# Attention block of a transformer layer: query projection as 4x4 by 4x4 blocks in 49 products, computed for all tokens ahead of the attention

## The chip, the cores and the metric

The kernel runs on one core of one Trainium2 chip. A core has a matrix engine (TensorE, PE in the profile), a vector engine (VectorE, DVE), an activation engine (ScalarE, ACT), a general engine (GpSimd, POOL) and a sync engine (SyncE, SP) that here only issues DMA transfers. Each engine works through its own instructions in order; semaphores tie them together. The metric is device time in microseconds (us), lower is better. The kernel before takes 1169.54 us, the median of three runs (1169.38 to 1170.08).

## The reference, cut to what matters

All arithmetic is fp32. There are 16 sequences of 128 tokens and a model width of 1024. Attention has 32 query heads of 32 columns in 8 key/value groups, so keys and values are 256 columns wide each.

```python
# _layernorm(x) = (x - mean) / sqrt(var + 1e-5)
h = _layernorm(x)                      # (16, 128, 1024)
query = h @ w_q.T                      # 1024 columns
key   = ctx @ w_k.T                    # 256 columns
value = ctx @ w_v.T                    # 256 columns
scores = einsum('bghnd,bgsd->bghns', query, key) / 32 ** 0.5
attention = softmax(where(mask, scores, finfo.min))
out = einsum('bghns,bgsd->bghnd', attention, value)
x = x + out @ w_out.T
h2 = _layernorm(x)
x1, x2 = split(h2 @ w12.T + b12)       # 2 x 1024 columns
x = x + (silu(x1) * x2) @ w3.T + b3
```

## The kernel before

**Tokens.** The 2048 tokens are two halves `T` = 0 and 1 of 1024 tokens (8 sequences `t` each). One half is two column blocks of 512 tokens, the widest matmul the kernel uses.

**Products in seven.** Every projection is a product of a 2x2-block left operand (weights) with a 2x2-block right operand (tokens), done by Winograd's scheme with 7 block products instead of 8. `seven_right` (L217) makes the differences of the right operand: four of shape 128x1024 in two pieces each, some on VectorE, the late ones on VectorE or GpSimd. `left_sums` (L245) makes the four sums of the left operand on GpSimd. `seven` (L263) runs the products in a given order: for each product a chain of matmuls into one PSUM bank (`chain`, L186), then the eviction. It uses four banks. Product 1 is copied by ScalarE (`p1`, L275), products 6 and 5 become `u1` and `u3` by two VectorE additions (L278, L280), and the result blocks come out by `done`. After each product `hook(j)` starts whatever is planned there: loads, sums, differences, statistics.

**Rounds.** `seven_round(T, k, R)` (L481) is one round: 7 products of 4 matmuls, 28 matmuls, each 128x128 weights by 128x512 tokens. Round `k` = 0 makes the keys of half `T`, `k` = 1 its values, `k` = 2 to 5 its queries, a quarter of the query columns each. The query weights are centred and scaled first (`centre`, L438), so that only 1/std of the layer norm is left for the scores. The centred weights are stored to DRAM and read again for half 1. `O_round(r)` (L605) is the output projection of two sequences, also 28 matmuls, with the residual added by `into` (L596).

**Order.** First the keys and values of half 0, interleaved; then its four query rounds, alone on the matrix engine; then the attention of half 0, and beside it the six rounds of half 1 (keys, values, four of queries); then the attention of half 1, and beside it output rounds 0 to 5. Output rounds 6 and 7, the second layer norm and the feed-forward part follow. `x_work` (L714) feeds the differences of the query rounds, `wo_work` those of the output rounds.

**Attention.** A unit is one sequence `t` and one half of the heads `gh`; a half `T` has 16 units. `scores` (L518) issues 16 small matmuls into four PSUM banks `s`. VectorE scales and masks each bank in place (L535) and takes the row maximum (L538), two banks at a time. ScalarE does 16 exponentials with row sums (L544). VectorE inverts the sums (L550) and GpSimd scales the probabilities `p` (L553). One unit later `flip` (L556) transposes `p` in four groups on the matrix engine, and VectorE copies each group to SBUF (`pT`, L561). Another unit later `values` (L564) multiplies with the values, and ScalarE copies the result (L575).

**How the two are interleaved.** The loop at L778 takes `share` us of round work per unit out of a `Stream` (L75): a quarter after the scores, 0.15 after `values`, 0.15 after each of the four flips. `share` is 147.0/16 in half 0 and (24.1*6 - 18)/16 in half 1. The matrix engine's order is fixed by the program in all parts (`manual_schedule`, L154); in the attention the order on VectorE, ScalarE, GpSimd and SP is chosen by a scheduler when the program is built.

**Buffers.** `psum` (L160) has 8 banks for everything: scores, flips, values and rounds. `units` (L157) has 44 buffers of 128x1024 fp32, `temps` 14 of 128x512. A new tile waits until the last user of its buffer is done.

**Feed-forward.** The product with w12 already uses the seven-product scheme twice: 4x4 by 4x4 blocks in 49 small products. A `step` (L937) is one inner set of 7 products of 2 matmuls. 28 steps go over 7 outer products times 4 groups of output rows. Partial results live in SBUF or in DRAM (`hold`, `store`, `fetch`, L907 to L916), and `gather` (L918) adds one to another with an accumulating DMA issued by GpSimd.

## Time and profile before

The profiled execution took 1167.91 us; its span from the first to the last instruction is 1166.1 us. That is 1.63 us below the median of the runs shown.

| what | where in the span, us |
|---|---|
| keys, values of half 0 | 8.6 to about 58 |
| queries of half 0 | about 58 to 153.0 |
| first scores of half 0 / of half 1 | 153.0 / 366.2 |
| last scores of half 1 | 548.5 |
| first matmul of the w12 steps | 639.3 |
| first matmul with w3 | 983.7 |

Engine totals over the span: PE 1156.3 us (99%), DVE 823.2 (71%), POOL 584.5 (50%), ACT 342.2 (29%). A fp32 matmul of these shapes is two PE instructions in the profile. Busy times of the matrix engine come from modelled ends, so its share says that it had work queued, and the chain of waits says better what it waited for. The granted clock of the matrix engine is 1.000 over the whole span.

### The profile page before, as it was taken

To read this page: it belongs to the slowest core of one execution; us is meant where nothing else is said; L and a number is where in the kernel's file an instruction comes from. 1 tells how busy PE (TensorE), PEld (TensorE's weight loads), DVE (VectorE), ACT (ScalarE), POOL (GpSimd) and SP (SyncE) were. 2 spreads that over 40 slices of the span, in tenths; PEclk is the share of its full clock that TensorE was granted. 3 is DMA by queue.
4 is the path that set the end of the run, shared out by engine and by line. 5 is a ranking of instruction groups with operands and counts; after the bars stand their busy time and mean duration, and the time that the engine had idled before them with its cause. 6 is when DMAs were issued, how large, how long until landed. Compare 5 with 4: busy or idle time off the path is not lost.

```text
span 1166.1 us, 13425 instructions
## 1 busy us (share of the span) xinstructions
PE 1156.3 (99%) x4288; PEld 541.0 (46%) x4288; DVE 823.2 (71%) x1194; ACT 342.2 (29%) x1325; POOL 584.5 (50%) x543
## 2 busy tenths in 40 slices
PE   9999999999999999999999999999999999999998
PEld 4444444444544455454454554444444444444443
DVE  4572368878678888888646446766777787978772
ACT  1120044555544464644261321110011022111111
POOL 5532255745356665556443358562523442548555
PEclk9999999999999999999999999999999999999999
DMA  9674342221215333133475789878834879272411
GB/s 366 249 281 169 125 146 91 91 91 55 91 55 199 127 109 128 55 128 109 162 278 209 277 333 318 231 246 252 173 106 157 221 203 277 91 270 91 162 73 72
DMA packets 65653, 200.13 MB, mean 172 GB/s; under 512 B 7088, under 2 KB 11184, under 8 KB 65584
## 3 DMA queue, kind: packets, MB, share of 16 engines
q1 hardware_dynamic: 60400, 180.93, 42.6%
q0 software_dynamic: 4320, 15.73, 7.2%
q10 hardware_dynamic: 864, 2.62, 0.6%
q8 instruction: 34, 0.56, 0.2%
q14 instruction: 35, 0.29, 0.1%
HBM read 127.95 MB, written 63.96 MB: 165 GB/s over the span
## 4 chain that ended last, share of the span: by engine, by line
PE 92%; DVE 4%; DMA 2%; issue 1%; ACT 0%; POOL 0%; SPq 0%; DVEq 0%; POOLq 0%; ACTq 0%
PE F_b L189 26%; PE Q_b L189 22%; PE O_b L189 17%; PE G_b L189 15%; PE pt L559 4%; PE s L526 3%; PE o L571 2%; PE xt L667 1%; DMA M<-U_dram 1%; DVE wo_T L233 1%; DMA ctx<-in_ctxT_dram 1%; DVE s L535 1%; DVE xT_T L233 1%; DMA OTr<-OT_dram 0%; DVE nmax L538 0%
## 5 line engine op out<-in xcount | busy, mean ns | idle before, releaser
L544 ACT ACTIVATE p<-s,nmax 128x128 f32<-128x128 f32 x512 | 181.4, 407 | 176.2 <-DVE nmax L538 168.7
L553 POOL TENSOR_TENSOR p<-p,inv 128x512 f32<-128x512 f32 x128 | 136.3, 1086 | 168.2 <-DVE inv L550 128.9
L189 PE MATMUL F_b<-X_T,L 128*128 128x512 f32 x304 | 135.7, 592 | 0.0
L544 ACT ACTIVATION_READ_ACCUMULATOR p<-s,nmax 128x1 f32 x512 | 126.3, 247 | 0.0
L189 PE MATMUL G_b<-w_R,A_L 128*128 128x512 f32 x256 | 114.4, 592 | 0.0
L535 DVE SCALAR_TENSOR_TENSOR s<-s,mr,drop 128x512 f32<-128x512 f32 x128 | 90.3, 751 | 24.6 <-PE s L526 24.5
L561 DVE COPY pT<-pt 128x512 f32<-128x512 f32 x128 | 84.4, 676 | 18.1 <-PE pt L559 17.1
L559 PEld LDWEIGHTS pt<-ident,p 128*128 128x128 f32 x512 | 63.6, 141 | 69.8 <-issue 63.5
L189 PEld LDWEIGHTS F_b<-X_T,L 128*128 128x128 f32 x304 | 57.4, 190 | 70.8 <-issue 69.4
L538 DVE TENSOR_REDUCE nmax<-s 128x4 f32<-128x512 f32 x128 | 81.8, 680 | 0.0
L559 PE MATMUL pt<-ident,p 128*128 128x128 f32 x512 | 76.9, 273 | 2.4 <-issue 2.4
L189 PEld LDWEIGHTS G_b<-w_R,A_L 128*128 128x128 f32 x256 | 48.6, 190 | 61.2 <-issue 59.6
L293 POOL TENSOR_TENSOR x<-x,G_n 128x512 f32<-128x512 f32 x36 | 49.9, 1413 | 49.4 <-DVE G_n L356 30.0
L374 ACT COPY G_c<-G_b 128x512 f32<-128x512 f32 x52 | 30.4, 585 | 142.3 <-PE G_b L189 141.1
L275 ACT COPY F_p<-F_b 128x512 f32<-128x512 f32 x28 | 16.4, 585 | 187.5 <-PE F_b L189 187.5
L950 DVE TENSOR_TENSOR M<-F_u,F_b 128x512 f32<-128x512 f32 x57 | 39.0, 685 | 44.8 <-PE F_b L189 43.1
L293 POOL TENSOR_TENSOR x<-x,G_c 128x512 f32<-128x512 f32 x36 | 53.8, 1512 | 32.5 <-ACT G_c L374 16.7
L189 PE MATMUL O_b<-wo_T,O_S 128*128 128x512 f32 x128 | 61.7, 601 | 0.0
L189 PE MATMUL O_b<-wo,O_S 128*128 128x512 f32 x128 | 61.6, 601 | 0.0
L189 PE MATMUL F_b<-xnT,L 128*128 128x512 f32 x128 | 60.8, 592 | 0.0
L189 PE MATMUL Q_b<-xT,wq 128*128 128x512 f32 x128 | 60.1, 597 | 0.0
L189 PE MATMUL Q_b<-xT_T,A_S 128*128 128x512 f32 x128 | 59.9, 598 | 0.0
(209 smaller groups left out, 2055.8 us busy)
## 6 DMA issues: line engine op xcount, KB each, us to landing
w<-in_w_dram SPq DMA_DIRECT2D x36, 512.0 KB, 6.8
xT<-in_xT_dram SPq DMA_DIRECT2D x16, 512.0 KB, 7.9
xs<-in_x_dram SPq DMA_DIRECT2D x16, 512.0 KB, 5.9
xp<-in_x_dram SPq DMA_DIRECT2D x16, 512.0 KB, 6.7
x_dram<-xp SPq DMA_DIRECT2D x16, 512.0 KB, 2.9
xn_dram<-xn SPq DMA_DIRECT2D x16, 512.0 KB, 2.9
xnr<-xn_dram SPq DMA_DIRECT2D x16, 512.0 KB, 5.7
h<-hT_dram SPq DMA_DIRECT2D x16, 512.0 KB, 6.0
```

The costliest lines, as they stand in the source:

```text
L189: nc.tensor.matmul(ps, lhsT, rhs, start=start and i == 0, stop=stop and i == len(pairs) - 1, skip_group_check=True,)
L233: eng.tensor_sub(t[e], a()[e], b()[e])
L293: (eng.tensor_add if op == "+" else eng.tensor_sub)(out, a, b)
L374: nc.scalar.copy(t, ps)
L526: nc.tensor.matmul(ps[gl][:, j, :], QT[T, c, gh * 2 + j // 2][rows, j % 2, toks], KT[T, c][rows, gh, toks], start=True, stop=True,)
L535: nc.vector.scalar_tensor_tensor(s, s, rstd, drop.unsqueeze(1).to_broadcast([P, HPG, S]), ALU.mult, ALU.add,)
L538: nc.vector.tensor_reduce(nmax[:, e], s, AX.X, ALU.max, negate=True)
L544: nc.scalar.activation(p[:, j, :], ps[gl][:, j, :], AF.Exp, bias=nmax[:, e, j : j + 1], accum_out=total[:, e, j : j + 1],)
L553: nc.gpsimd.tensor_mul(p, p, inv[:, e].unsqueeze(2).to_broadcast([P, HPG, S]))
L559: nc.tensor.transpose(pt[:, j, :], p[:, j, :], ident)
L561: nc.vector.tensor_copy(pT, pt)
L950: nc.vector.tensor_add(dst, s, ps)
```

## The change

1. The query rounds go. The queries of all 2048 tokens are made in one piece between the keys and values of half 0 and its attention: weights in 2 groups `g` of 512 query columns, 4x4 blocks of the weights (128 rows each) by 4x4 blocks of the tokens (512 each), 7 outer times 7 inner products. One `q_step` is 7 products of 2 matmuls; there are 14 steps, 196 matmuls.
2. VectorE makes the outer differences of the tokens (`q_outer_right`, 16 of 128x1024) and the inner ones (`q_inner_right`, 28 of 128x1024). All token blocks are loaded once, 16 of 512 KB.
3. GpSimd makes the outer sums of the weights (`q_outer_left`, 8 instructions of 128x512 per group) and the inner ones (`q_inner_left`, 4 of 128x256 per step). Outer sums go through DRAM and come back two steps ahead of their use.
4. Partial results: outer products 1, 2, 3 and 5 have their own tiles; 6, 7 and 4 are added to a tile `u` by two VectorE additions per block. Two sums pass through DRAM (`q_store`, `q_fetch`), and three times per group `q_gather` adds two tiles by an accumulating DMA of GpSimd. Finished queries of half 1 and some of half 0 are stored to DRAM and loaded before their attention (`q_home`).
5. Statistics of half 0 move into the steps, those of half 1 into its key and value rounds and output rounds 0 and 1.
6. Beside the attention of half 0 now run: keys and values of half 1, output rounds 0 and 1. Beside that of half 1: output rounds 2 to 5. `share` becomes 98.0/16 and (24.1*4 - 12)/16.
7. The stage of the steps has its order written out on all five engines; the attention stages keep the scheduler as before.

```diff
+class Pieces:
+    def __init__(self, made):
+        self.made = made
+    def __getitem__(self, k):
+        return [self.made[k]]
...
-    wq_dram = [tc.dram_tile([P, 2, KC, P], F32, name=f"wq_dram_{m}") for m in range(4)]
...
+    OUTER = (1, 2, 3, 6, 5, 7, 4)
+    INNER = (1, 5, 6, 7, 2, 3, 4)
+    Q_STEPS = [(g, i) for i in OUTER for g in range(2)]
+    def load_xq(K, C, h, c):
+        xq[2 * K + h, 2 * C + c] = load(xT[C][2 * K + h, c], [2, 512], f"xq_{2 * K + h}_{2 * C + c}")
+    def q_outer_right(i, h, c):
+        B11, B12, B21, B22 = (xq.get((2 * K + h, 2 * C + c)) for K in range(2) for C in range(2))
+        y = Y.setdefault(i, {})
+        if i in (1, 2, 3):
+            y[h, c] = {1: B11, 2: B21, 3: B22}[i]
+            return
+        out, x, z = {
+            5: (B11, B12, B11), 6: (None, B22, Y.get(5, {}).get((h, c))), 7: (B12, B22, B12),
+            4: (B21, B21, Y.get(6, {}).get((h, c))),
+        }[i]
+        y[h, c] = out if out is not None else unit([2, 512], f"Y6_{h}_{c}")
+        nc.vector.tensor_sub(y[h, c], x, z)
+    def q_inner_right(i, k):
...
+        nc.vector.tensor_sub(r[k], a, b)
+    def q_outer_left(g):
+        A11, A12, A21, A22 = (q_part(g, R, K) for R in range(2) for K in range(2))
+        S = {k: unit([2, 2, 2, P], f"QS{k}_{g}") for k in (5, 6, 7, 3)}
+        for k, a, op, b in (
+            (5, A21, "+", A22), (6, S[5], "-", A11), (3, A12, "-", S[6]), (7, A11, "-", A21),
+        ):
+            for h in range(2):
+                x, z = (t[:, h] if t in (S[5], S[6]) else t[h] for t in (a, b))
+                put(nc.gpsimd, S[k][:, h], x, op, z)
+        for k in (2, 3, 6, 5, 7, 4):
+            t = q_dram[g, k] = tc.dram_tile([P, 2, 2, 2, P], F32, name=f"QS{k}_dram_{g}")
...
+    def q_gather(g, to, frm):
+        for r in range(2):
+            o, x = ((q_sum_dram if k in ("U", "V") else q_sum)[g, k][r] for k in (to, frm))
+            nc.gpsimd.dma_start(o, x, accum_op=ALU.add)
+    def q_step(n):
+        g, i = Q_STEPS[n]
         def done(rc, s, ps):
+            dst, u, v = (q_sum[g, k][rc[0]][:, rc[1]] if (g, k) in q_sum else None for k in (i, "u", "v"))
+            if dst is None:
+                nc.vector.tensor_add(u, u, ps)
+                if s is not None:
+                    nc.vector.tensor_add(u, u, s)
+                return
             if s is None:
                 nc.scalar.copy(dst, ps)
             else:
                 nc.vector.tensor_add(dst, s, ps)
+            if i == 5:
+                nc.vector.tensor_add(v, v, ps if s is None else dst)
...
+    def q_plans():
+        for n, (g, i) in enumerate(Q_STEPS):
+            if i != 1:
+                q_at(n - 2, 3, q_load_left, g, i)
+            for e, k in enumerate((1, 5, 6, 7, 3)):
+                q_at(n - 1, 3 + e if n else min(5 + e // 2, 7), q_inner_left, g, i, k)
...
+            if i == 1:
+                q_at(0 if g else -1, 7, q_outer_left, g)
+                q_at(n + 1, 2, q_store, g, i, "U")
...
+        for i, hcs, ks in (
+            (1, [(-1, 5)] * 4, ((-1, 6), (-1, 6), (-1, 7), (0, 1))),
+            (2, [(0, 6)] * 4, ((0, 7), (1, 1), (1, 2), (1, 7))),
+            (5, [(2, 1), (2, 2), (3, 1), (3, 2)], ((6, 7), (7, 1), (7, 2), (7, 7))),
+            (3, [(2, 6)] * 4, ((2, 7), (3, 4), (3, 7), (4, 4))),
+            (6, [(4, 1), (4, 2), (4, 7), (5, 1)], ((5, 2), (5, 7), (6, 1), (6, 2))),
+            (7, [(8, 1), (8, 2), (8, 7), (9, 1)], ((9, 2), (9, 7), (10, 1), (10, 2))),
+            (4, [(10, 7), (11, 1), (11, 2), (11, 4)], ((11, 7), (12, 1), (12, 2), (12, 4))),
+        ):
...
     def O_round(r):
-        if r + 1 < B // 2:
+        if EARLY <= r < B // 2 - 1:
             load_pair(r + 1)
...
-            if j == 5 and r + 1 < B // 2:
+            tick()
+            if j == 3 and r < EARLY:
+                load_pair(r + 1)
+            if j == (6 if r < EARLY else 5) and r + 1 < B // 2:
                 left_O(r + 1)
+            if r < 2 and j in (1, 3):
+                load_xs(NT + 4 + 2 * r + j // 2)
+            if r < 2 and j in (4, 6):
+                q_stats(NT + 4 + 2 * r + j // 2 - 2)
...
-    stream.add(*(seven_round(0, k, x_R[0]) for k in range(2, 6)))
-    stream.finish()
+    with tc.manual_schedule(engines={ENGINES.PE, ENGINES.DVE, ENGINES.Activation, ENGINES.Pool, ENGINES.SP}):
+        stream.add(*(q_step(n) for n in range(len(Q_STEPS))))
+        stream.finish()
+    feeds["ctx_1"].finish()
...
-            stream.add(*(seven_round(1, k, ctx_R[1] if k < 2 else x_R[1]) for k in range(6)))
-            share = 147.0 / NT / GH
+            stream.add(*(seven_round(1, k, ctx_R[1]) for k in range(2)))
+            stream.add(*(O_round(r) for r in range(2)))
+            share = 98.0 / NT / GH
         else:
-            stream.add(*(O_round(r) for r in range(EARLY)))
-            share = (24.1 * EARLY - 18.0) / NT / GH
+            stream.add(*(O_round(r) for r in range(2, EARLY)))
+            share = (24.1 * (EARLY - 2) - 12.0) / NT / GH
```

A plan entry (n, j) means: in step n, after its product number j; n = -1 is the last of the key and value rounds of half 0.

## The prediction

> **What bounds the kernel now.** I read the chain of waits first, then busy times by stage, then one attention unit in the timeline.

> ```profile
> PE 92%; DVE 4%; DMA 2%; issue 1%; ACT 0%; POOL 0%; SPq 0%; DVEq 0%; POOLq 0%; ACTq 0%
> ...
> 74.96 78.11 PE Q_b L189 x182
> ```
> ```profile
> 58.00:153.00 95.00, 95.00 (x225) 42.00 (x223) 41.87 (x69) 11.46 (x23) 31.87 (x35) 1.00 0.51 184
> 153.00:366.20 213.20, 210.64 (x1221) 104.20 (x1220) 173.43 (x290) 106.66 (x544) 111.45 (x99) 1.00 0.25 88
> 366.20:548.50 182.30, 181.56 (x1117) 89.97 (x1116) 152.01 (x275) 95.86 (x504) 114.35 (x111) 1.00 0.34 126
> ```
> The chain is the matrix engine nearly everywhere. Its second line gives the price of a matmul: 78.11 / 182 = 0.429 us per instruction, two per matmul, 0.858 us. In the stage table the columns are length, then busy PE, weight loads, DVE, ACT, POOL. VectorE is at 44% in the query stage, 81% and 83% in the two attention stages. So the matrix engine leads, with VectorE not far behind beside the attention.

> ```profile
> 451.13 1.17 PE L526 MATMUL s<-K,Q 32*128 32x128 f32 x32
> 452.32 1.42 DVE L535 SCALAR_TENSOR_TENSOR s<-s,mr,drop 128x512 f32<-128x512 f32 x2 [1.25 <-PE s L526]
> ...
> 454.42 0.37 ACT L544 ACTIVATE p<-s,nmax 128x128 f32<-128x128 f32 x1 [2.59 <-DVE nmax L538]
> ...
> 460.30 0.30 ACT L544 ACTIVATION_READ_ACCUMULATOR p<-s,nmax 128x1 f32 x1
> 460.63 0.20 DVE L550 RECIPROCAL inv<-sum 128x8 f32<-128x8 f32 x1 [0.95 <-ACT p L544]
> 460.75 1.24 DVE L561 COPY pT<-pt 128x512 f32<-128x512 f32 x2
> 462.52 0.68 DVE L561 COPY pT<-pt 128x512 f32<-128x512 f32 x1
> 463.11 1.16 PE L526 MATMUL s<-K,Q 32*128 32x128 f32 x30
> ```
> This is one unit of half 1: 463.11 - 451.13 = 11.98 us from scores to scores. From the scores to the end of the last exponential it is 460.60 - 451.13 = 9.47 us, if VectorE is free when the scores come. The slack is 2.5 us. I hold on to it because of the eight banks: in both programs as built, the next unit's scores wait for banks that the last exponentials, or VectorE's copies of the flips, still hold. So 9.47 plus about 0.1 for the semaphore, 9.6 us, is a floor of the unit's period, whatever the matrix engine has to do.

> **The change, part by part.**

> **1. Matmuls: -24.0 us.** Eight query rounds of 28 matmuls go (224), 14 steps of 14 come (196). 28 x 0.858 = 24.0 us. The built programs agree: 2480 matmul instructions before, 2452 after.

> **2. The query stage: +10 us (4 to 25).** It grows from 4 rounds to 14 x 14 x 0.858 = 168.2 us of matmuls. VectorE's work in it: 41 of the 44 differences of 128x1024 (3 come earlier) at 1.65 us, 67.7; `u1` and `u3`, 28 x 0.69 = 19.3; 74 block additions (24 into own tiles, 42 into `u`, 8 into `v`) x 0.69 = 51.1; the eight sequences' statistics (16 x 0.673 + 8 x 0.51) = 14.8; centring of group 1, 8 x 0.61 = 4.9; four differences of the context for the next stage, 6.6. Sum 164.4 us, 98% of the matmuls beside it. It is uneven: steps of outer products 6, 5, 7 and 4 have nine additions (6.2), about three differences (5.0) and, up to step 10, statistics (1.8), 13.0 us against 12.0. The eight steps from number 6 on fall behind by some 7 us. The first six carry 10 us each, but what they save can't be used ahead, since the differences are at fixed places. When outer product 7 begins, its second and third inner difference are made at the end of step 9 and in step 10, directly ahead of the products that use them; a late VectorE is then a waiting matrix engine. The feed-forward steps are the nearest row: 392 x 0.858 = 336.3 in 344.4 us, 8 us lost in 28 steps with VectorE at 68%. Below nothing is excluded: no matmul became shorter. I take 7 for the overload and 3 for the start: SP's stores of the outer sums wait for GpSimd (16 instructions of 1.27 us), and behind them in SP's queue stand the loads of the last token blocks, which VectorE needs in step 2. ScalarE (11%) and the accumulating DMAs (12 of them; 6 to 9 us to landing, with a step or more between) lie under the matmuls; if such a DMA is late by x, VectorE waits x.

> [...]

> ```profile
> L860 DVE TENSOR_TENSOR X_T<-xnT,X_T x12: 1212/1222/3311, 620.6 to 924.9; 128x1024 f32<-128x1024 f32 x12
> L860 DVE TENSOR_TENSOR X_T<-xnT,xnT x10: 1218/1222/3362, 617.1 to 888.9; 128x1024 f32<-128x1024 f32 x10
> ```
> The same difference takes 1.22 us in the middle and up to 3.36 us (min, median, max); the page's means are 1.63 and 1.68. [...] All 44 differences have two SBUF inputs and GpSimd sums weights beside them. Left alone, 44 x 1.22 = 54 us; by the mean row, 73. [...] I take the mean row, since GpSimd is busy about 45% in the feed-forward and about 40% in the new stage.

> **3. Attention of half 0: +21.6 us (5 to 35).** The period was 213.2 / 16 = 13.3 us. 49 us of rounds go: 13.3 - 49/16 = 10.25 us for the matrix engine. VectorE: 173.4, less four token differences (7.8), twelve query blocks (8.0) and two rounds' `u` (2.7), plus eight output blocks (5.4), four more sequences' statistics for the second norm (5.5) and 1 of small ones: 166.8 / 16 = 10.4 us per unit, above the matrix engine's 10.25. Two queues, each full, that wait for each other in order can't both be kept full. What a late VectorE instruction does can be seen:

> ```profile
> 349.96 5.88 DVE L233 TENSOR_TENSOR wo_T<-wo,wo_T 128x1024 f32<-128x1024 f32 x2
> 350.42 1.17 PE L526 MATMUL s<-K,Q 32*128 32x128 f32 x32
> 355.77 0.75 DVE L535 SCALAR_TENSOR_TENSOR s<-s,mr,drop 128x512 f32<-128x512 f32 x1
> ```
> Two differences stand ahead of the masking, which starts 5.35 us after the scores instead of 1.19; that unit took 15.75 us even with today's slack. I take 11.6 us per unit, 1.35 x 16.

> **4. Attention of half 1: +19.5 us (3 to 30).** Period 182.3 / 15 = 12.15. `share` falls from 7.91 to 5.28, so 9.5 us for the matrix engine, already under the floor of 9.6. VectorE: 152.0 less seven output blocks, six statistics and four `u`, 140.5 / 15 = 9.4. I chained four units by hand in the built order of VectorE, with the durations above. Sequence 10, first half: two additions, two statistics and three copies still stand ahead of its masking, which begins 3.3 us after its scores; exponentials end at 11.6; the next scores wait for them: 11.75. Its second half: an inversion that waits for the last exponential (10.45) stands ahead of three copies, to 12.0, and the next scores wait for the third: 12.05. The two units before it come to 9.6 and 9.9. Mean 10.8, 1.3 x 15 = 19.5.

> **5. The rest: 0.** The queries' stores and loads (SP has 435 transfers for 391) land units ahead of use; DMA was at 0.25 and 0.34 beside the attention and 0.51 in the query stage. Should loads wait for one of the 44 buffers, the first output round starts late, 5 us. The tail after the last scores has 12 instead of 18 us of rounds to cover the last flips; these need the last scores' probabilities about 13 us after the scores, and come later than that.

> **Sum.** -24.0 + 10 + 21.6 + 19.5 = +27.1. The profiled execution of 1167.9 becomes 1195.0 (its span 1166.1 becomes 1193.2); with the 1.6 us by which the median lies above it, **1197 us**.

> **Clock.** The granted clock is 1.00 in every row. [...]

> **Rivals.**
> - *The cover holds; faster.* VectorE's queue keeps up, as it did at 83% without visible waits; the mechanism is that banks come free in time because the scheduler puts the masking first. Then half 1 pays only the floor and the flips that wait for exponentials (9.9 - 9.5) x 15 = 6, half 0 only its one unit with differences, 4, the steps 4: -24 + 14 = -10, 1159 us. It wins while the three stages together lose under 24 us. Against it: VectorE's sum per unit already equals the matrix engine's.
> - *The head of the query stage.* SP stands behind GpSimd's outer sums, the token loads land 7 to 8 us late in step 2, VectorE never makes it up: 15 more in that stage, 1212 us. For it: SP's order is written out; against it: the banks of two steps lie between.
> - *The matmuls go but the units overlap badly throughout*: 12.2 us in half 0 and 11.5 in half 1: +31 + 30 + 10 - 24, 1217 us.

> That the change doesn't do what it says is excluded by the count of matmuls.

> **Chances.** The forecast with its bounds (1175 to 1208) 0.53; head of the query stage 0.13; units worse 0.14; faster 0.14; around no change 0.06. Range 1168 to 1224. Within 0.2% (2.3 us) is what a measurement can't tell from no change: 0.04; slower 0.82, faster 0.14.

> **What would show it.** Period between scores: 10.25 or below in half 0 and 9.6 in half 1 says the cover holds; 11 to 12 says I am right. VectorE's share in these stages should be 88 to 95%, and its inversions and masking should end the waits of the matrix engine there. The stage of the steps should last 172 to 193 us, with waits for differences in steps 8 to 13. A granted clock below 0.98 there, or waits for loads, would mean another cause than mine.

## The result, and the profile after

The changed kernel takes **1206.63 us** (median of 4 runs, 1201.86 to 1208.91) against 1169.46 us for the kernel before in the same comparison (4 runs, 1169.17 to 1170.08): 1.031 times the time, 95% interval 1.028 to 1.035. The profiled execution took 1208.91 us, its span is 1207.0 us. The forecast was 1197 us, 1195.0 for the profiled execution, with 1168 to 1224 as the range.

The page of the changed kernel, its busy times and its chain of waits:

```profile
PE 1165.1 (97%) x4232; PEld 540.9 (45%) x4232; DVE 907.4 (75%) x1288; ACT 345.5 (29%) x1331; POOL 623.4 (52%) x575
...
PE 63%; DVE 11%; ACT 7%; DMA 5%; issue 3%; POOL 2%; SPq 0%; ACTq 0%; DVEq 0%; POOLq 0%
```

The matrix engine was 92% of the chain and is now 63%; VectorE and ScalarE, 4% together before, now carry 18%. The matrix engine is busy for 1165.1 us although 28 matmuls are gone: before it was 1156.3. So its instructions have become longer somewhere. The stage table (start:end, length, busy time of PE, weight loads, DVE, ACT and POOL, granted clock, DMA share, GB/s) shows where: query stage, attention of half 0, attention of half 1.

```profile
57.95:247.10 189.15, 175.92 (x401) 75.99 (x399) 155.59 (x188) 17.54 (x34) 96.08 (x89) 0.96 0.83 279
247.10:433.37 186.27, 172.48 (x1106) 87.03 (x1105) 160.76 (x286) 103.16 (x538) 106.68 (x99) 0.96 0.34 125
433.37:594.88 161.51, 154.16 (x1023) 76.30 (x1022) 141.38 (x261) 93.51 (x496) 86.42 (x89) 0.97 0.22 83
```

The third number from the end is the granted clock, as a share of full speed. It was 1.00 in every row before; now it is 0.96 to 0.97 in all three stages that the change touches, and 1.00 in the rest. The mean over the span is 0.984: as the clock in the records is either full or half, 2 x 0.016 x 1207 = 39 us of the span ran at half clock (37.5 us in six stretches, and the very end).

| stage | before | forecast | measured |
|---|---|---|---|
| query stage | 95.0 | 178.2 | 189.15 |
| attention, half 0 (16 periods) | 213.2 | 185.6 | 186.3 |
| attention, half 1 (15 periods) | 182.3 | 162.0 | 161.5 |
| from the last scores to the end | 617.6 | 609.4 | 612.1 |

The forecast of the last row is what is left of the forecast span of 1193.2 us after the others and the first 58 us.

The two stages of attention came out as forecast, to 0.7 us. But they are not made as forecast. The periods from scores to scores, read off the starts of the score matmuls in the timeline, are:

```
half 0:  8.2 11.0 11.2 10.3 10.3 11.3 17.8 10.7 10.2 12.1 10.4 11.5 10.3 10.7 10.4 20.0
half 1: 10.5 10.6 10.0  9.4 11.0 11.1 12.4 10.3  9.6  9.9 16.2  9.6 10.8  9.9 10.2
```

Most units are near the matrix engine's own 10.25 us in half 0 and near the floor of 9.6 us in half 1; three long units of 17.8, 20.0 and 16.2 us lie 24 us above that, over half of the 41 us that the two stages lost against their matrix work. Each has its own cause, and all three have a low clock (the last but two numbers: 0.81, 0.83, 0.79):

```profile
309.26:327.06 17.80, 14.27 (x72) 7.33 (x71) 16.74 (x25) 6.65 (x34) 12.59 (x9) 0.81 0.46 184
413.42:433.37 19.95, 15.69 (x76) 7.98 (x75) 14.85 (x29) 6.48 (x35) 14.18 (x17) 0.83 0.18 70
538.19:554.39 16.20, 13.34 (x69) 6.78 (x68) 10.33 (x20) 7.53 (x40) 7.15 (x11) 0.79 0.44 159
```

**The unit at 413 us**, in the timeline:

```profile
421.28 1.26 POOL L303 TENSOR_TENSOR O_S<-OTr,O_S 128x512 f32<-128x512 f32 x1
422.63 0.24 POOL L218 TENSOR_SCALAR is_a<-mr 128x8 f32<-128x8 f32 x1
422.91 0.21 ACT L219 ACTIVATE is_a<-is_a 128x8 f32<-128x8 f32 x1 [10.39 <-POOL is_a L218]
423.15 0.21 ACT L220 ACTIVATE mr<-is_a 128x8 f32<-128x8 f32 x1
423.27 0.35 ACT L728 ACTIVATE p<-s,nmax 128x128 f32<-128x128 f32 x1
...
424.85 1.09 PE L743 MATMUL pt<-ident,p 128*128 128x128 f32 x4 [4.21 <-POOL mr L224]
```

ScalarE stands idle for 10.39 us ahead of a logarithm that belongs to the other half's layer norm (`inv_std`). It waits for an addition of epsilon on GpSimd, and GpSimd has four sums for an output round in front of that. Behind the logarithm stand this unit's exponentials, whose row maxima were ready at 419.64 (the first pair of reductions starts at 418.37 and takes 1.27). They begin at 423.27, 3.6 us late; the matrix engine waits 4.21 us for a bank that they hold. The profile names another instruction of the layer norm for that wait (`mr`, done at 424.50), but the fourth exponential, with which the first bank is free, ends at 424.75, 0.10 us before the flip.

**The unit at 538 us** has the same chain from the second layer norm, with VectorE as the engine that is held:

```profile
539.04 2.04 POOL L737 TENSOR_TENSOR p<-p,inv 128x512 f32<-128x512 f32 x2 [1.24 <-DVE inv L734]
...
540.20 0.90 DVE L211 COPY mr_f<-mv_f 128x2 f32<-128x2 f32 x1
...
541.19 0.23 POOL L218 TENSOR_SCALAR is_f<-mr_f 128x4 f32<-128x4 f32 x1
...
543.06 0.16 DVE L827 SCALAR_TENSOR_TENSOR mr_f<-mr_f 128x4 f32<-128x4 f32 x1 [1.96 <-POOL mr_f L224]
543.14 1.41 DVE L719 SCALAR_TENSOR_TENSOR s<-s,mr,drop 128x512 f32<-128x512 f32 x2
```

A 0.16 us instruction that nobody needs before the end of the attention waits 1.96 us, and the masking (L719), due at about 539.4 (1.19 us after the scores), is behind it. The chain began late too: its copy of 128x2 numbers (L211) took 0.90 us, and ended with GpSimd's instruction beside it.

**The unit at 309 us** is of the kind that the prediction had seen in the kernel before: weight differences ahead of the masking.

```profile
309.26 1.72 PE L710 MATMUL s<-K,Q 32*128 32x128 f32 x15
...
312.17 3.08 DVE L243 TENSOR_TENSOR wo_T<-wo,wo_T 128x1024 f32<-128x1024 f32 x1
...
315.17 1.41 DVE L719 SCALAR_TENSOR_TENSOR s<-s,mr,drop 128x512 f32<-128x512 f32 x2
```

The masking starts 5.9 us after the scores. The one difference took 3.08 us while GpSimd made two of the same weights.

**The head of the query stage.** Step 2 of the stage, in the timeline:

```profile
81.33 2.85 SPq L517 DMA_DIRECT2D QS_dram<-QS  x4
...
84.23 2.42 SPq L520 DMA_DIRECT2D QS_dram<-wq  x2
...
90.72 2.07 SPq L193 DMA_DIRECT2D xq<-in_xT_dram  x3
...
95.38 1.23 DVE L488 TENSOR_TENSOR xq<-xq,xq 128x1024 f32<-128x1024 f32 x1 [7.68 <-DMA xq<-in_xT_dram]
...
100.01 0.69 DVE L290 TENSOR_TENSOR Q_u<-Q_b,Q_u 128x512 f32<-128x512 f32 x1
...
100.81 3.75 PE L199 MATMUL Q_b<-xq,QI 128*128 128x512 f32 x4 [6.91 <-POOL QI L303]
```

SP stands behind GpSimd's outer sums (10.6 us ahead of one store) and issues the stores of group 1 at 81.3 to 86.7; only then come the loads of the last token blocks. VectorE waits 7.68 us for the first of them and has `u1` and `u3` (L290) behind it in its queue. The next product needs the bank that `u3` reads. The profile names GpSimd's `QI` as the releaser; in the program the waiting matmul waits for three things, a load, those sums, done at 86.6, and `u3`, done at 100.70, 0.11 us before the matmul starts. Four instructions then take 3.75 us instead of 1.88: half clock.

### The profile page after: what moved, and what is told of

It is laid out like the page before. It is cut to its first block, busy times and chain, and to the rows that moved or that the text cites. A ratio compares the mean times of both kernels' runs of the same rounds, so it can differ in the third digit from the quotient of the medians.

```text
span 1207.0 us, 13599 instructions
## 1 busy us (share of the span) xinstructions
PE 1165.1 (97%) x4232; PEld 540.9 (45%) x4232; DVE 907.4 (75%) x1288; ACT 345.5 (29%) x1331; POOL 623.4 (52%) x575
## 4 chain that ended last, share of the span: by engine, by line
PE 63%; DVE 11%; ACT 7%; DMA 5%; issue 3%; POOL 2%; SPq 0%; ACTq 0%; DVEq 0%; POOLq 0%
PE F_b L199 23%; PE G_b L199 15%; PE Q_b L199 10%; PE O_b L199 9%; ACT p L728 7%; PE pt L743 3%; DMA M<-U_dram 2%; DVE s L719 2%; PE s L710 2%; PE o L755 1%; DVE pT L745 1%; DVE nmax L722 1%; DVE xq L488 1%; DMA S6r<-S_dram 1%; DMA w<-in_w_dram 1%
## 5 line engine op out<-in xcount | busy, mean ns | idle before, releaser
L737 POOL TENSOR_TENSOR p<-p,inv 128x512 f32<-128x512 f32 x128 | 133.8, 1068 | 156.2 <-DVE inv L734 134.2
L743 PE MATMUL pt<-ident,p 128*128 128x128 f32 x512 | 81.0, 284 | 16.7 <-ACT p L728 7.6
L719 DVE SCALAR_TENSOR_TENSOR s<-s,mr,drop 128x512 f32<-128x512 f32 x128 | 90.1, 749 | 8.7 <-PE s L710 8.7
L745 DVE COPY pT<-pt 128x512 f32<-128x512 f32 x128 | 81.7, 673 | 12.1 <-PE pt L743 12.0
L199 PE MATMUL Q_b<-Y_T,QI 128*128 128x512 f32 x152 | 68.3, 594 | 2.2 <-DVE Y_T L496 2.2
L199 PE MATMUL O_b<-wo_T,O_S 128*128 128x512 f32 x128 | 67.5, 628 | 1.6 <-ACT p L728 1.6
L199 PE MATMUL O_b<-wo,O_S 128*128 128x512 f32 x128 | 64.4, 612 | 0.3 <-ACT p L728 0.3
L199 PE MATMUL O_b<-wo,OTr 128*128 128x512 f32 x112 | 57.2, 609 | 0.7 <-ACT p L728 0.7
```

Of the source, the lines that this page charges most:

```text
L199: nc.tensor.matmul(ps, lhsT, rhs, start=start and i == 0, stop=stop and i == len(pairs) - 1, skip_group_check=True,)
L719: nc.vector.scalar_tensor_tensor(s, s, rstd, drop.unsqueeze(1).to_broadcast([P, HPG, S]), ALU.mult, ALU.add,)
L737: nc.gpsimd.tensor_mul(p, p, inv[:, e].unsqueeze(2).to_broadcast([P, HPG, S]))
L743: nc.tensor.transpose(pt[:, j, :], p[:, j, :], ident)
L745: nc.vector.tensor_copy(pT, pt)
```

## The experiments

Each time is a median, with the lowest and the highest in brackets; behind it stands the ratio to the kernel before on the same chip, with its 95% interval. The kernel before took 1169.1 to 1170.5 us there. The last four experiments ran on other chips than most of their bases, so differences of 1 us between them say nothing.

### Stores of the outer sums one step later

```diff
-        for k in (2, 3, 6, 5, 7, 4):          # in q_outer_left
...
+    def q_keep_left(g, *ks):
...
+        for k in ks:
...
+                q_at(0 if g else -1, 7, q_keep_left, g, *((2,) if g else (2, 3, 6, 5, 7, 4)))
+                if g:
+                    q_at(1, 7, q_keep_left, g, 3, 6, 5, 7, 4)
```

> The changed kernel, with one thing moved: the stores of group 1's outer sums (all but the one needed next) come in SP's queue after the last token loads and the load of the next left block, a step later. Theory (queue order at the head): the matrix engine's 6.9 us gap in step 2 is SP standing behind GpSimd's sums, and the half clock that follows costs 3 us more; without it VectorE is in time until step 5, so the query stage (189 us from its first product to the first scores) shrinks by 7 to 10 us, the whole from about 1207 to 1197-1200. Rival (VectorE's total work sets the stage): the wait comes back in the later steps, the gaps after step 6 grow from 5 to over 10 us, and the whole gains under 3 us.

Measured: **1193.67 us** (1189.72 to 1195.54), 1.020 times the kernel before (1.018 to 1.023), 13 us less than the changed kernel. The query stage takes 179.1 us, from 55.70 to the first scores at 234.80, instead of 189.15: 10 us. The waits of the matrix engine in it are (total, times, longest), first in the changed kernel, then in this run:

```profile
PE Q_b L199 <- POOL QI L303: 6.9, 1, 6.9
PE Q_b L199 <- DVE Y_T L496: 5.0, 3, 2.7
```

```profile
PE Q_b L199 <- DVE Y_T L496: 4.9, 3, 2.7
```

The 6.9 us wait is gone, and the three late ones are what they were; one more, of 1.3 us, is in both. The theory holds for the stage; VectorE did not bring the wait back. The whole gained 3 us more than was expected: in the profiled execution (1189.72 us) the attention is 6.7 us shorter too: the same long units took 16.6, 18.6 and 13.7 us instead of 17.8, 20.0 and 16.2, with three half-clock stretches in the whole run for six, though nothing in them was changed.

### Inverse deviations on other engines

```diff
-        nc.gpsimd.tensor_scalar(v, y, EPS, None, ALU.add)
+        nc.vector.tensor_scalar(v, y, EPS, None, ALU.add)
...
-            nc.vector.scalar_tensor_tensor(mf[:, 2, :], mf[:, 0, :], -1.0, mf[:, 1, :], ALU.mult, ALU.mult)
+            nc.gpsimd.tensor_mul(mf[:, 2, :], mf[:, 0, :], mf[:, 1, :])
+            nc.gpsimd.tensor_scalar(mf[:, 2, :], mf[:, 2, :], -1.0, None, ALU.mult)
```

> The changed kernel, with the inverse deviations re-routed and no work left out: the addition of epsilon that ScalarE's logarithm waits for goes from GpSimd to VectorE, and the shift that VectorE computes from the finished chain goes to GpSimd. Theory (a foreign chain in a queue): the two long units of attention, 19.95 us (ScalarE holds its exponentials behind a logarithm that waits for GpSimd) and 16.2 us (VectorE holds the masking behind a shift that waits for GpSimd), fall to 10-12 us, so the whole falls by 11 to 15 us to 1192-1197; the half-clock stretches in those two units go with them. Rival (VectorE is overloaded beside the attention, and the long units are only where the backlog shows): the units move the loss to neighbours, which grow from 10.5 to 11.5 us, and the whole changes by less than 4 us.

Measured: **1200.15 us** (1197.05 to 1202.55), 1.026 (1.024 to 1.028): 6.5 us less. The two units fall from 19.95 to 13.42 us and from 16.20 to 11.72. The unit after the first grows from 10.5 to 12.2 and the next from 10.6 to 11.1. So the foreign chains were real waits, worth 6.5 and 4.5 us with the half-clock stretches that lay in these units, of which the neighbours take 2.1 back. The gain of the whole, 6.5 us, lies between the two expectations. The rest of the expected gain is lost elsewhere: from the last scores to the end this run took 616.5 us instead of 612.1, with a 1.9 us wait for GpSimd and a half-clock stretch in the feed-forward part that the changed kernel did not have.

### Matmuls put into the waits

```diff
+            if name == "Q2" and i == 3:       # in seven
+                for _ in range(7):
+                    nc.tensor.matmul(banks[1], *product(A, R, 2)[0], start=True, stop=True, skip_group_check=True)
...
+        for _ in range({(2, 0): 4, (6, 1): 4, (10, 0): 2, (12, 0): 3}.get((t, gh), 0)):   # in values
+            nc.tensor.matmul(o, ident, KT[T, c][:, 0, :], start=True, stop=True, skip_group_check=True)
```

> The changed kernel plus 20 matmuls of 128x512 (17 us of matrix engine time at 0.858 us) whose results are overwritten unread: seven ahead of the product that waits in step 2, and four, four, two and three ahead of the values of the units in which the clock fell. They lie in the stretches in which the matrix engine only waits. Theory (the clock falls because of the waits): the half-clock stretches in these five places disappear, 12 to 15 us of slow matmuls go, the mean granted clock rises from 0.984 to 0.995 or more, and the whole falls by 8 to 14 us though there is more work. Rival (the clock is no part of the loss, the waits alone are): the time stays within 3 us of 1207; if the filling is mis-placed it is up to 10 us slower.

Measured: **1201.05 us** (1198.71 to 1203.97), 1.027 (1.025 to 1.029), clock 0.996: with 17 us of additional matmuls the kernel is 5.6 us *faster*. So the clock is part of the loss, which is a causal answer, not only a correlation. But the size is under what was expected. In the profiled execution four of the five filled places gained: about 2.4 us at the head of the query stage (this run was 0.8 us ahead of the changed kernel just before the wait and 3.3 us ahead behind it) and 2.4, 2.4 and 1.9 us in the three long units. At the fifth, the 12.4 us unit, there was hardly a wait to fill: its half-clock stretch stayed, and it grew to 14.2 us. Two units that were not filled lost 4.1 us (11.0 to 12.9, 10.5 to 12.8), the first with a new half-clock stretch that came after a wait of 1.95 us. And at full clock the long units still take 15.4, 17.5 and 14.3 us: most of their length is the wait itself.

The first scores come 4.2 us earlier (242.9 for 247.1). 1.7 of these come from no filled place. The late wait of 2.71 us for a difference is in both runs, first the changed kernel, then this one:

```profile
231.47 2.75 PE L199 MATMUL Q_b<-Y_T,QL 128*128 128x512 f32 x4 [2.71 <-DVE Y_T L496]
```

```profile
228.17 1.98 PE L199 MATMUL Q_b<-Y_T,QL 128*128 128x512 f32 x4 [2.71 <-DVE Y_T L499]
```

Only in the first does half clock follow: the same four instructions take 2.75 us instead of 1.98. The experiment on the clock below shows why.

### One output round fewer beside half 1

```diff
-            share = (24.1 * (EARLY - 2) - 12.0) / NT / GH
+            share = (24.1 * 3 - 12.0) / NT / GH
```

> The changed kernel with one round's worth of output matmuls (24.1 us) taken out of half 1 of the attention and left to run after it: the matrix engine's work for a unit of half 1 falls from 9.5 to 8.0 us. Theory (a floor of about 9.6 us from scores through exponentials to the release of banks): the ordinary unit falls only from 10.4 to 9.6-10.0, so the half gains 6 to 12 of the 24 us and the whole becomes 12 to 18 us slower. Rival (VectorE's additions for the rounds set the unit's length): the unit falls in proportion, to 8.9-9.3, and the whole is 0 to 6 us slower.

Measured: **1217.68 us** (1215.95 to 1222.91), 1.041 (1.039 to 1.043), 11 us slower than the changed kernel, just under the 12 to 18 that were expected. Half 1 takes 151.6 us instead of 161.5, but 6 of these 10 are the long unit, which fell apart since the norm's chain came elsewhere. The mean period is 151.6 / 15 = 10.11 us; the ordinary periods of the changed kernel have (161.5 - 16.2) / 14 = 10.38. 1.5 us less of matrix work in each unit shortens it by 0.27 us. So the matrix work is not what sets the unit's length, and the rival, with units of 8.9 to 9.3 us, is excluded. The floor stands as a mean only: single units of this run took 8.7 and 9.3 us.

### Both mends together

> The late stores of the outer sums and the re-routed inverse deviations together, each as measured alone (1193.7 and 1200.2 us). Theory (two separate waits, 13 and 6.5 us): they add, 1186 to 1189 us, the long units of attention stay at 13.4 and 11.7 us or below, and the query stage at 177 us. Rival (both only hand their backlog on to the same later place): 1191 us or more.

Measured: **1189.29 us** (1187.55 to 1190.80), 1.017 (1.015 to 1.019). The gains were 13.0 and 6.5 and together 17.3: they nearly add. Half-clock stretches fell to two. This kernel is the base of the next ones.

### Statistics of half 0 in steps 2 to 5

```diff
-            q_at(t + 2, 1, load_xs, t)
-            q_at(t + 3, 4, q_stats, t)
+            q_at(t // 2 + 1, 5 + t % 2, load_xs, t)
+            q_at(t // 2 + 2, 4 + 2 * (t % 2), q_stats, t)
```

> The kernel with both mends, and the loads and statistics of half 0's sequences moved from one per step in steps 3 to 10 to two per step in steps 2 to 5 (the same instructions). Theory (the sum of the prediction: steps from number 6 on hold 13.0 us of VectorE work, the first six only 10): the gaps of 0.5, 1.8 and 2.7 us in steps 11 to 13 and the half-clock stretch after the last one go, the query stage falls from 177 to 170-172 us, the whole by 5 to 7 us. Rival (the late differences wait for something else, a load or GpSimd's sums): the gaps stay, and the whole moves by less than 1.5 us, or gets slower because the early steps have more DMA.

Measured: **1187.47 us** (1186.11 to 1188.55), 1.8 us less than its base, the kernel with both mends; the intervals (1.014 to 1.017 against 1.015 to 1.019) overlap. The waits for inner differences fall only from 4.9 to 3.7 us and the longest, 2.7, stays. In this run no half clock followed it, which alone is worth up to 1.7 us. Neither side got its numbers: where the statistics stand hardly matters.

### Preparation of the output weights spread out

```diff
+        if T == 1:
+            if (k, j) == (0, 1):
+                feeds["wo"] = Feed(wo_work, 0)
+            feeds["wo"].give(1 + k)
         if (T, k) == (1, 1):
-            if j == 1:
-                feeds["wo"] = Feed(wo_work, 2)
-            feeds["wo"].give(2)
```

> The kernel with both mends, and the preparation of the output weights begun one round earlier and spread over 14 places of the rounds instead of 7 (the same instructions). Theory (the 17.8 us unit of half 0 comes from two pairs of weight differences ahead of one masking on VectorE, 5.3 us after the scores): with the pairs in different units each costs 1 to 2 us at most, the long unit falls from 16.6-17.8 to 11-13 us and the whole by 3 to 6 us. Rival (the total VectorE work of half 0 counts, not its place): the long unit's loss spreads to two or three others, the sum of the 16 periods stays within 2 us.

Measured: **1189.13 us** (1188.88 to 1189.99), no change. The 16 periods of half 0 sum to 179.1 us instead of 178.6. The long unit went from 16.6 to 15.4 us and its two neighbours from 10.3 and 11.3 to 11.4 and 11.9. With the weight differences gone from the queue, statistics and additions stood there instead, and the masking was still 4.7 us late. The rival's forecast came true: moving this work from one place changed nothing. That the amount of VectorE's work counts is left to the run with the copies.

### What makes the clock fall

```diff
+        m = (n - 3) % 7 + 1
+        if j == 4 and 3 <= n < 24:            # after product 4 of feed-forward steps 3 to 23
...
+            nc.tensor.matmul(ps, ident, ident, start=True, stop=True)
+            for _ in range(2 * m):
+                nc.scalar.copy(t, ps)
+            nc.tensor.matmul(ps, ident, t, start=True, stop=True)
```

> A measurement, on the changed kernel: in 21 feed-forward steps the matrix engine is made to wait in the middle of the step for 2, 4, 6, 8, 10, 12 or 14 chained ScalarE copies of 128x128 (about 0.3 us each, so 0.8 to 4.5 us of wait; each length three times, 12 us apart). It adds work that nobody reads, so its total time says nothing. Theory (the clock is decided on a fixed grid of 3.41 us, and a cell in which more than about 1.9 us is waiting makes the next cell half clock): waits up to 1.7 us never lower the clock, waits of 2.0 to 3.4 us do in some places and not in others, by where they lie in the grid, waits over 4 us always. Rival (an idle stretch of 3.4 us is needed): no wait below 3.4 us lowers it.

Measured (one execution, 1289.01 us with the added waits): the waits were 0.65 to 4.21 us long. How many of the three of each length were followed by half clock:

| wait, us | 0.65 | 1.25 | 1.84 | 2.43 | 3.03 | 3.62 | 4.21 |
|---|---|---|---|---|---|---|---|
| half clock after it | 0 | 0 | 0 | 1 | 3 | 3 | 3 |

In the stage table, the stretch behind a wait of 2.43 us that ended at 882.55, one of 2.43 that ended at 996.25, one of 1.84 and one of 3.03 (last but two: the clock):

```profile
882.55:885.90 3.35, 3.35 (x6) 1.80 (x7) 0.00 (x0) 0.00 (x0) 0.00 (x0) 0.52 0.10 40
996.25:999.60 3.35, 3.35 (x10) 1.68 (x11) 0.69 (x1) 0.00 (x0) 0.00 (x0) 1.00 1.08 335
981.09:984.50 3.41, 3.41 (x10) 1.74 (x11) 0.75 (x2) 0.58 (x1) 0.00 (x0) 1.00 0.89 285
...
1012.20:1015.60 3.40, 3.40 (x6) 1.40 (x6) 0.00 (x0) 0.00 (x0) 0.00 (x0) 0.53 0.11 20
```

The same wait of 2.43 us costs nothing in one place and in another halves the clock for the 3.4 us that follow: six matmul instructions in 3.35 us instead of ten. All half-clock stretches in the records of these runs, but for the end of a run, are 3.41 us long or a multiple of it, and their starts within a run are whole multiples of 3.41 us apart: in the changed kernel 96.02, 232.55, 317.88, 423.70, 498.79 and 546.58, which is 40, 25, 31, 22 and 14 times 3.41 us from one to the next. So in these records half clock begins on a fixed grid of 3.41 us, and what went with it was how much of one cell is waiting. Laid over this grid, the wait of 2.43 us that ended at 882.55 lies in one cell; the one that ended at 996.25 is cut into 1.52 and 0.91. The 21 waits sort without an exception: where one cell had 2.38 us or more of waiting the next ran at half clock, and where no cell had more than 1.85 us it did not. The same count, by the records of the matmuls, over the 13 traces of the changed kernel and its variants, for cells at full clock away from the two ends of a run: all 39 cells with 1.95 us or more of waiting were followed by half clock, and only 6 of the 4386 with less, two of them with 1.92 and 1.93. The other four cells are mostly score matmuls. In the changed kernel alone five cells with 2.12 to 3.05 us of waiting were all followed, and of 332 with 1.58 or less one was. The rival, which needs 3.4 us of idle time in one piece, is excluded by the four waits of 2.43 and 3.03 us.

### The last of four copies on ScalarE

```diff
-        nc.vector.tensor_copy(pT, pt)
+        if gl == 3:
+            nc.scalar.copy(pT, pt)
+        else:
+            nc.vector.tensor_copy(pT, pt)
```

> The kernel with both mends (1189.3 us; 16 periods of half 0 sum to 178.6 us, 15 of half 1 to 158.3), with the last of the four copies of flipped probabilities of each unit made by ScalarE instead of VectorE: 0.67 us less for VectorE in every unit, the same for ScalarE more. Theory (VectorE's amount of work limits both halves, as the prediction has it): half 0 falls by 5 to 9 us, towards 16 x 10.25 = 164 at most, half 1 by 2 to 6, where the last copy no longer delays the next scores; the whole becomes 1176 to 1183. Rival (the limit is the chain from scores through exponentials to free banks, which ScalarE's extra copy lengthens): half 0 changes by less than 2 us and half 1 gets 3 to 9 us longer.

Measured: **1180.87 us** (1180.10 to 1180.99), 1.009 (1.007 to 1.011), 8.4 us less than its base. The two halves:

```profile
236.55:411.87 175.32, 167.94 (x1105) 83.80 (x1104) 152.04 (x273) 111.55 (x553) 105.59 (x98) 1.00 0.36 130
411.87:565.25 153.38, 148.16 (x1024) 74.36 (x1023) 133.93 (x248) 100.63 (x510) 87.02 (x90) 1.00 0.25 91
```

Half 0 falls by 3.3 us (178.6 to 175.3), all of it in the long unit (16.6 to 12.8, of which up to 1.7 us is a half-clock stretch that went with the wait); its ordinary units hardly move. Half 1 falls by 4.9 (158.3 to 153.4), spread over most units; that ScalarE's extra copy would lengthen it is excluded. So VectorE's amount of work does bound half 1, through the copies that hold banks, and in half 0 only the one unit in which it had a backlog. Of the runs that compute everything this is the fastest, and still slower than the kernel before.

### The second context block spread over steps 7 to 13

```diff
-        for j in range(1, 8):
-            q_at(11, j, feed_ctx)
-            q_at(12, j, feed_ctx)
-            q_at(13, j, feed_ctx)
+        for n in range(7, 14):
+            for j in (2, 4, 7):
+                q_at(n, j, feed_ctx)
```

> The kernel with both mends and the early statistics (1187.5 us), with the loads and differences of the second context block spread over steps 7 to 13 of the query stage instead of standing in steps 11 to 13 (the same instructions). Theory (the two gaps left in steps 11 to 13, 1.0 and 2.7 us, are the context differences standing ahead of the inner differences that the next product needs): the gaps go, the stage ends 2 to 4 us earlier, 1183.5 to 1186. Rival (VectorE is simply full from step 6 to the end, wherever they stand): other gaps of the same sum appear in steps 8 to 11, and the time stays within 1.5 us of 1187.5.

Measured: **1191.67 us** (1187.95 to 1194.95), 1.018 (1.015 to 1.022), not faster than its base, the run with the early statistics (1187.47 us). The waits of the matrix engine in the stage:

```profile
PE Q_b L199 <- DVE Y_T L496: 3.7, 2, 2.7
PE Q_b L199 <- DVE Q_u L290: 3.5, 2, 2.6
```

The old wait stays, and a new one of 2.6 us comes beside it. The rival holds for the waits: from step 6 on VectorE is full wherever the differences stand. Its time, within 1.5 us of the base, was missed: the median is 4.2 us longer, the profiled execution (1189.44 us) 1.9.

### All of it

> All of these at once: late stores, re-routed deviations, early statistics, spread context block, and the last copy on ScalarE. If each mends its own wait the times add: 1187.5 less 2 to 4 for the context block and less 5 to 12 for the copies, 1172 to 1181 us. That would still be slower than the kernel before (1169.1). If VectorE is full whatever the order and ScalarE's copy lengthens the unit, 1187 or more.

Measured: **1182.31 us** (1180.51 to 1184.96), 1.011 (1.008 to 1.014). Between the two forecasts (1172 to 1181, and 1187 or more), and no better than the copies alone on the two mends: what the copies gain is kept, what the two moves within the query stage were to gain is not there.

### 18 block additions left out

```diff
                 nc.vector.tensor_add(u, u, ps)
-                if s is not None:
-                    nc.vector.tensor_add(u, u, s)
                 return
```

> The kernel with both mends and the last copy on ScalarE (1180.9 us; first product of the query stage to first scores about 178.6 us, 1.3 + 5 us of gaps in it), with 18 of the block additions of steps 6, 7 and 10 to 13 left out: the second summand of the running sum is never added, so the queries are not the reference's. VectorE has 18 x 0.69 = 12.4 us less to do in these six steps, 2 us of 13 in each. Theory (VectorE's amount of work from step 6 on makes the remaining gaps): the gaps of steps 11 to 13 and the half-clock stretch after them go, first scores come 5 to 7 us earlier, the whole is 1174 to 1177. Rival (the differences wait for GpSimd's sums, a load or the accumulating transfers): the gaps stay, and the time is within 2 us of 1180.9.

Measured: **1175.19 us** (1172.43 to 1177.64, 9 runs), 1.0037 (1.0026 to 1.0048), 5.7 us less than its base, the kernel with both mends and the copy. Even without this work the kernel before is faster. The waits in the query stage, first of this kernel, then of its base:

```profile
PE Q_b L199 <- DVE Y_T L496: 1.4, 3, 1.0
```

```profile
PE Q_b L199 <- DVE Y_T L496: 4.9, 3, 2.7
```

The first scores come 5.1 us earlier (231.43 for 236.55), and no half-clock stretch is left before the end. Together with the two moves that changed little or nothing, this shows the cause in the late part of the stage: the amount of VectorE's work, not its order, makes those waits.

## Why the prediction came out as it did

**The sign was right, and the mechanism in the main.** Twenty-eight matmuls went, 24 us, and three stages gave back more. But two things that the prediction had named as signs of another cause in the stage of the steps, a granted clock below 0.98 and waits for loads, were there: the clock was 0.96, and VectorE waited 7.68 us for a load. VectorE's share was 86% and 88% beside the attention, just under the 88 to 95 forecast, and the matrix engine's long waits there ended mostly with ScalarE's exponentials. By the steps of the prediction, in the profiled execution:

| term | forecast | measured | how measured |
|---|---|---|---|
| matmuls | -24.0 | -24.0 | count |
| query stage over its matmuls | +10 | +21.0 | 189.15 - 168.2 |
| half 0 | +21.6 | +22.1 | 186.3 - (213.2 - 49) |
| half 1 | +19.5 | +19.0 | 161.5 - (182.3 - 39.75) |
| rest | 0 | +2.7 | 612.1 - 609.4 |
| sum | +27.1 | +40.8 | 1208.9 - 1167.9 = 41.0 |

**Step 2, the query stage, is the term that was too small**, by 11 us. Its first part, "3 for the start", had the mechanism word for word: SP behind GpSimd's outer sums, token loads behind SP, VectorE behind the loads, in step 2. It was mis-sized: the matrix engine waited 6.9 us there and then ran at half clock for another 5.4, which costs about 2.7; moving the stores gave 10 us of that stage. This was priced as a rival too, with 15 us, and for the reason against it ("the banks of two steps lie between") the forecast took the small value. That reason fails because VectorE works in order: `u3` of the current step stood behind the late differences, so the wait reached the matrix engine within one step. The other part, 7 us for VectorE's overload from step 6 on, was 5.0 us of waits and one half-clock stretch after them, 1.7 us at most: right, and the run without 18 additions shows the mechanism. What remains of the 21.0 us is the wait of 1.3 us and some 3 us of transposes and small matmuls that stand in the stage and not in the sum of 168.2. VectorE's busy time was 155.6 us for 164.4 forecast, 5 us of it because the differences were cheaper: the rows of L488 and L496 give 67.3 us for 44, 1.53 us each, where the mean row had promised 1.65. They were longer beside GpSimd: the 15 differences with no GpSimd instruction beside them took 1.22 us each, the 29 with one 1.71 in the mean and 2.28 at the most. In the kernel before, the 10 of L860 without one took 1.22 us as well, the 18 with one 1.80 in the mean and 3.36 at the most; none of the new ones took as long as that.

**Steps 3 and 4 were right in their sums and wrong in their shape.** "11.6 us per unit" and "10.8" were measured as 11.64 and 10.77. I had meant all units a little longer. In fact the ordinary units of half 0 have (186.3 - 17.8 - 20.0) / 14 = 10.6, close to the matrix engine's own time, and two long ones make the rest. One of these is the backlog of VectorE that I had pointed to. The other, and the long unit of half 1, are chains of the layer norm through three in-order queues, which the prediction didn't have at all; the statistics appear in it only as VectorE time. So part of the agreement is luck: the overload was smaller than forecast (one copy less per unit gave 3.3 and 4.9 us), and something not foreseen filled the difference. The floor of 9.6 us in half 1 holds for the mean: with 1.5 us less matrix work it stayed at 10.1, though single periods went to 8.7.

**The sum has no term for the clock, and that is wrong.** That the waits I foresaw would leave it at 1.00 was my assumption, and no run shows it. The records have six stretches of half clock, 37.5 us in all, five of them behind waits of 2.6 to 6.9 us and one with hardly a wait. In the run on the clock three waits of 3.03 us out of three were followed by half clock, and in the count over the traces so was every cell with 1.95 us or more of waiting. What it cost here lies, as an estimate, between the 5.6 us that filling five places brought in net and about 15 us (half of what is left of 37.5 us without some 8 us in which the matrix engine was waiting anyway). The clock also goes with the spread: the four runs of the changed kernel lie between 1201.9 us at a clock of 0.991 and 1208.9 at 0.984.

**Step 5, the rest,** is right to 2.7 us. In the experiments that did not touch it this part varied between 612 and 616.5 us, in part by single waits for GpSimd or VectorE; why these come and go is open. Open too is why the half-clock stretch at 498 us of the changed kernel comes after waits of only 0.57 us. 2.1 us of the cell before it are score matmuls, as in the three cells of other runs that fell in the same way, but other cells with as many were not followed, and whether these matmuls count less for the clock was not tried.

**The rivals.** The head of the query stage came true as a place, inside the forecast's sum rather than as a case of its own. "The cover holds" fell: no version of the changed kernel reached the time of the kernel before. With both late waits mended and a copy moved, 1180.9 us, its query stage still had 179.2 us (57.35 to 236.55) for 168.2 of matmuls and half 1 10.2 us per unit for 9.5. What makes the last 0.6 us per unit above the floor is not shown. "The units overlap badly throughout" (12.2 and 11.5 us) fell too.

## What to carry to other kernels

Taking matmuls out of a stage gains only if the work that they covered is still covered: per stage, add up the second engine's time and the shortest chain through the buffers, and compare these with what is left for the matrix engine. A short chain that crosses several in-order queues (here a layer norm's seven tiny instructions, worth 6.5 and 4.5 us in two units) costs what stands *behind* its waiting members, so look at each member's queue, not at its 0.2 us. And a wait of the matrix engine can cost more than its length: in the changed kernel waits of 2.57 to 6.91 us came with stretches of 3.41 to 10.24 us at half clock.

## What the runs showed of the hardware

Tiny VectorE copies ended with GpSimd's instruction beside them. Of the changed kernel's 32 copies of 128x2 numbers (L211), the 20 with no GpSimd instruction beside them took 0.12 to 0.17 us; the 12 with one took up to 1.03 us, and each ended 0.02 to 0.03 us after a GpSimd instruction did.

The releaser that the profile names for a wait with several conditions can be one that was done 14 us before: GpSimd's sums at 86.6 for a matmul at 100.8, which in truth waited for VectorE.
